# Row products by table, bias and batch in one matmul, token groups in serpentine order, and a new order of pieces behind the sort

## The chip, the cores and the metric

The kernel runs on one core of one Trainium2 chip. The metric is the device time of one execution in microseconds (us). Three runs of the kernel before took 981.32, 984.67 and 981.96 us; their median is 981.96. One further execution was recorded by the hardware profiler: it took 977.43 us, and its profile is what the prediction reads.

The engines are named as in the profile: PE (TensorE: matrix products), PEld (its weight loads), DVE (VectorE), ACT (ScalarE), POOL (GpSimd, which here also issues the indirect DMAs that gather rows), and SP (SyncE, which here only issues DMAs).

## The reference, cut to what matters

`x` is 16 batches of 512 tokens of 512 numbers, all float32. Each token has a pathway (of 500), a compartment c (of 5), and a mask value m (0 or 1, in a table of three scales).

```python
def _ln(x, g, b): return (x - mean(x)) * rsqrt(var(x) + 1e-5) * g + b
def _mlp_ln(s, W1, b1, W2, b2, g, b): return _ln(silu(s @ W1 + b1) @ W2 + b2, g, b)

h = _ln(x, pw_g[pathway], pw_b[pathway])
h = _ln(h, cp_g[c], cp_b[c])
t = _ln(x, tm_g[c], tm_b[c])
s = _ln(x, ms_g[m], ms_b[m])
mem, noi, res = (x + _mlp_ln(state, ...)[:, None, :] for each of three states of the batch)
w = softmax(aw)                                            # six weights
cat = concat([w[0]*h, w[1]*t, w[2]*mem, w[3]*noi, w[4]*res, w[5]*s])   # 3072 wide
out = x + _mlp_ln(cat, int_W1, int_b1, int_W2, int_b2, int_g, int_be)
```

## The kernel before, in words

The 8192 tokens are 64 tiles of 128; four tiles are a window, and there are 16 windows. `D` is 512, cut into `NC` = 4 blocks of 128.

**The first layer by groups.** The tables of `t` and `s` depend on (m, c) alone. There are `NR3` = 3 by `NR5` = 5, `NG` = 15 groups (the mask takes two of the three). The kernel sorts all tokens by group on the chip (a loop of one-hot products on PE, L710 to L733) and then gathers each tile of sorted tokens by an indirect DMA on POOL. The tokens of a tile then mostly share their group, so the weights of `t` and `s` with their gains can be one 512 by 512 block per tile, `vs`: ACT scales `ws` (`s_part`, `sp`, L213) and DVE adds the scaled `wt` (`build`, `bd`, L222). So `layer1` (L315) has three blocks of four matmuls for each tile: X (the tokens, against the summed weights of the three states, `wx_`), V (the normalized tokens against `vs`) and H (the twice normalized tokens against `wh_`). The pieces are `lX`, `lV`, `lH`.

**What is added to the rows.** What depends on the batch (16, through the three states) and on the group, and the bias `b1`, is one of 240 rows (`NB1` = 15 x 16). They are made in two halves of `HB` = 120 (`rows_product`, `rp`, L1071): one matmul of a one-hot `pick` against the summed tables `br2`, four matmuls against the identity that bring the bias (`b1r`), and one matmul of another one-hot against the batch rows `br`. `br2` is the copy (`br2`, L999) of what `table_products` (`tb`, L992) summed up; `br` is the copy (`cr`, L1042) of what `cond_product` (`cm`, L1035) summed up from the states; both copies are on ACT. The halves are copied (`rc`) and written by SP to two tables in memory, `rows_1` and `rows_2` (`ro`, L1082); the rows of a tile are gathered from `rows_2` (`ga`, L228) and added behind layer 1 (`ha`, L323).

**Extra tiles.** Where a group ends within a tile, the tile is built with the weights of one group, and the tokens of the other are corrected. The 15 groups have 14 boundaries. Half tiles of 64 tokens at the boundaries are put together in pairs, two to an extra tile, plus one (`ex.0`, against `ws`) for the two boundaries between mask values, where c changes too: `NX` = 7, and eight extra tiles, in two sets e0 and e1 of up to four. Each is gathered (`gx`), normalized, multiplied by the difference of the two groups' gains (`gr`, `mt`), turned (`tr`, `sE`), and multiplied by `wt` or `ws` (`extra`, `ex`, L1097: four matmuls). The product is added to the gathered rows (`ea`, `ee`) and written to `rows_1` or `rows_2` (`extra_out`, `eo`, L1110), from where the corrected tokens gather it by the indices that `kinds` (L891), `extra_adds` (L1057) and `add_rows` (`ar`, L1116) work out.

**Turning.** The products need the tokens' numbers on the partitions. DVE transposes 32 by 32 (`turn`, L182; pieces `tx`, `tv`, `th`, `tz`), and SP moves the 64 KB strips into place (`spread_row`, L187): one row group of a block is a piece `sX`, `sV`, `sH` or `sZ` with four DMAs. In window 0, X is turned by PE instead (`xt`, copies `xv`).

**The second layer** is seven products of quarters for each two tiles (`seventh`, `q7`, L397) with sums and differences of the turned rows on POOL (`zs`, L375), or plainly four matmuls a tile (`layer2`, `l2`, L336) in the first windows and the last.

**The order.** No scheduler decides it: each engine gets its instructions in the order of three written lists. `ORDER` holds the start, up to and into the first windows; `WINDOW` is run for w = 0 to 14 with the suffixes o, p, c, n and m for the windows w-2, w-1, w, w+1 and w+2 (a piece that ran already is left out); `LAST` is the last window and the end. In a piece, `lX.c.2` is block X of layer 1 for tile 2 of the current window. Pieces in `ORDER` that are not layer work: `lw` loads `w2` (L1140), `wm` sums its columns on ACT (`w2_means`, L1129: six ACT instructions), `wk` weighs `wx_` on DVE, `wh` weighs `wh_` on ACT (L979), `xs` are the row sums of a tile on ACT, `nv` and `xn` its two norms, `fn` and `fp` the second norm of H.

## Time and profile before

| | us |
|---|---|
| three runs | 981.32, 984.67, 981.96 |
| profiled execution | 977.43 |
| its span (first to last instruction) | 975.6 |
| PE busy | 951.4 |
| PE weight loads busy | 500.4 |
| DVE busy | 811.8 |
| POOL busy | 661.9 |
| ACT busy | 573.8 |

The granted clock of PE is 0.992 of full speed over the span. A busy PE need not be PE at its peak, since the ends of its pipelined matmuls are modelled. The profile counts a float32 matmul as two instructions. A row of the time line has start, duration, engine, line, operation, output and inputs by the program's names, sizes and the number of instructions taken together; a bracket at its end names the wait ahead of it. A row of the stretches has the stretch, its length, the busy time of PE, PEld, DVE, ACT and POOL with the number of instructions, PE's clock, the share of DMA time and GB/s. `SPq` is the queue in which SP issues DMAs. The 64 tiles need 504, 512 and 512 matmul instructions in blocks V, X and H of the first layer.

### The profile page before, as it was taken

The page shows a single profiled execution, that of the slowest core. Times are in us where ns is not written, and L with a number is a line of the kernel's source. Part 1 is how long each engine was busy: PE and PEld are TensorE (multiplying, and loading weights), DVE is VectorE, ACT ScalarE, POOL GpSimd, SP SyncE. Part 2 cuts the span into 40 slices and gives each one's busy share as a digit, 9 for nine tenths or more (in the row PEclk, how much of TensorE's full clock was granted, in tenths as well). Part 3 has the DMA queues.
Part 4 walks back from the last instruction along what each step waited for, and adds up shares of the span by engine and source line. Part 5 has one row for each costly group of instructions (what it writes and reads, how often), then busy time and mean ns, then how long its engine had stood idle before and what let it go on. Part 6 is the DMA issues. An engine that isn't in the chain of part 4 may idle for free. (4 is left out here: it accounts for less than half of the span.)

```text
span 975.6 us, 11492 instructions
## 1 busy us (share of the span) xinstructions
PE 951.4 (98%) x2921; PEld 500.4 (51%) x2921; DVE 811.8 (83%) x1402; ACT 573.8 (59%) x1190; POOL 661.9 (68%) x683
## 2 busy tenths in 40 slices
...
GB/s 277 211 259 236 270 262 217 147 228 192 206 189 184 190 196 168 213 202 193 227 189 203 176 197 174 198 183 195 215 195 219 186 185 188 198 180 190 131 84 97
DMA packets 92044, 191.47 MB, mean 196 GB/s; under 512 B 25332, under 2 KB 25332, under 8 KB 91980
## 3 DMA queue, kind: packets, MB, share of 16 engines
...
## 5 line engine op out<-in xcount | busy, mean ns | idle before, releaser
L320 PE MATMUL p<-vs,cV 128*128 128x512 f32 x504 | 225.7, 592 | 0.0
L320 PE MATMUL p<-wx__82,cX 128*128 128x512 f32 x512 | 224.9, 592 | 0.0
L320 PE MATMUL p<-wh__83,cH 128*128 128x512 f32 x512 | 223.3, 592 | 0.8 <-DMA cH<-rH 0.7
L226 DVE SCALAR_TENSOR_TENSOR vs<-wt,sct,vs 128x512 f32<-128x512 f32 x252 | 186.8, 805 | 1.6 <-ACT vs L220 1.6
L220 ACT ACTIVATE vs<-ws,scs 128x512 f32<-128x512 f32 x252 | 164.0, 711 | 7.6 <-PE p L320 3.6
L320 PEld LDWEIGHTS p<-wh__83,cH 128*128 128x128 f32 x512 | 97.1, 190 | 123.9 <-issue 118.0
L320 PEld LDWEIGHTS p<-wx__82,cX 128*128 128x128 f32 x512 | 97.2, 190 | 122.8 <-issue 116.4
L320 PEld LDWEIGHTS p<-vs,cV 128*128 128x128 f32 x504 | 95.8, 190 | 109.5 <-issue 93.0
L497 POOL DMA_INDIRECT out<-yb,tok x64 | 80.1, 1251 | 71.5 <-DVE yb L462 21.9
L471 ACT ACTIVATE junk<-yb 128x512 f32<-128x512 f32 x64 | 40.4, 631 | 116.0 <-DVE yb L435 92.4
L327 ACT ACTIVATE add<-add 128x512 f32<-128x512 f32 x64 | 39.4, 626 | 93.9 <-DVE add L324 93.9
L158 POOL DMA_INDIRECT add<-rows,i_add x64 | 73.6, 1149 | 19.4 <-issue 10.4
L158 POOL DMA_INDIRECT pw<-in_pw,i_pw x64 | 71.8, 1122 | 19.6 <-issue 16.9
L309 POOL TENSOR_TENSOR xbs<-xbs,rows 128x512 f32<-128x512 f32 x64 | 84.0, 1313 | 1.0
L158 POOL DMA_INDIRECT xbs<-in_x,tok x64 | 67.1, 1049 | 25.7 <-issue 12.3
L158 POOL DMA_INDIRECT cp<-cp_rows,i_cp x64 | 63.0, 984 | 20.5 <-issue 18.6
L260 ACT ACTIVATE xm<-xbs,nmx,rsx 128x512 f32<-128x512 f32 x64 | 51.7, 810 | 38.1 <-DVE rV L184 38.1
L484 POOL TENSOR_TENSOR rsy<-vey,mhalf 128x4 f32<-128x4 f32 (+1 forms) x15 | 21.3, 1423 | 77.4 <-DVE vey L479 77.3
L283 DVE TENSOR_TENSOR pw<-xn,pw 128x512 f32<-128x512 f32 x64 | 45.5, 710 | 26.5 <-DMA pw<-in_pw,i_pw 26.2
L238 ACT ACTIVATE junk<-xbs 128x512 f32<-128x512 f32 x72 | 44.9, 623 | 33.2 <-DMA xbs<-in_x,tok 30.9
L292 POOL TENSOR_TENSOR rsh<-veh,mhalf 128x1 f32<-128x1 f32 x64 | 43.3, 681 | 25.9 <-DVE vea L244 16.4
L296 ACT ACTIVATE pw<-pw,rsh 128x512 f32<-128x512 f32 x64 | 44.1, 711 | 27.5 <-POOL rsh L292 27.3
...
## 6 DMA issues: line engine op xcount, KB each, us to landing
cV<-rV SPq DMA_DIRECT2D x256, 64.0 KB
cH<-rH SPq DMA_DIRECT2D x256, 64.0 KB
cZ<-rZ SPq DMA_DIRECT2D x256, 64.0 KB
cX<-rX SPq DMA_DIRECT2D x240, 64.0 KB
...
```

The lines of the kernel that those rows point to most:

```text
L158: nc.gpsimd.indirect_dma_start(dst, None, table, bass.IndirectOffsetOnAxis(ap=idx, axis=0), **kw)
L220: nc.scalar.activation(v[:, c], ws[:, c], AF.Identity, scale=scs[:, c, g, w : w + 1])
L226: nc.vector.scalar_tensor_tensor(v[:, c], wt[:, c], sct[:, c, g, w : w + 1], v[:, c], ALU.mult, ALU.add)
L238: nc.scalar.activation(junk, x, AF.Identity, accum_out=sums[:, 0, j : j + 1])
L260: nc.scalar.activation(t, st["xb"][:, j, :], AF.Identity, bias=st["nm"][:, j : j + 1], scale=st["rs"][:, j : j + 1])
L283: nc.vector.tensor_mul(pw[:, :D], st.pop(("xn", j)), pw[:, :D])
L292: nc.gpsimd.tensor_tensor(rs, st.pop(("ve", j)), mhalf[:, :1], ALU.pow)
L296: nc.scalar.mul(pw[:, :D], pw[:, :D], st.pop(("rs", j)))
L309: nc.gpsimd.tensor_add(st["xb"][:, j, :], st["xb"][:, j, :], rows[:, 2, :])
L320: nc.tensor.matmul(st["p1", g], st["c" + blk][:, g, c, :], m[:, c, :], start=(blk == "X" and c == 0), stop=(blk == "H" and c == NC - 1))
L471: nc.scalar.activation(junk, yb[:, j, :], AF.Square, accum_out=st["ssy"][:, j : j + 1])
L497: nc.gpsimd.indirect_dma_start(out_rows, bass.IndirectOffsetOnAxis(ap=tok[:, j, w : w + 1], axis=0), yb[:, j, :], None)
```

## The change

It has three parts.

1. The tables, the bias and the batch rows are summed in one PSUM tile, `pb`. The columns of the tables are moved behind the 16 of the batches, a fourth plane of `tabs` holds the bias in column L - 1 = 31, and four matmuls of 32 by 128 against the identity add it. The copy `br2` is gone, `cr` copies all; `pick` is a single one-hot sum with up to four ones in a column, and `rows_product` is one matmul for each half. `cond_affine` now works on 16 of the 32 columns.

2. The groups are ordered as a serpentine: where m is odd, c runs backwards. At the boundary between two mask values c is then the same on both sides. `NX` becomes 6, there are seven extra tiles (`ex.0` to `ex.6`), and `rows_2` holds 14 half tiles behind the 240 rows. `extra_out` writes two halves for each extra tile to `rows_2`, the first one to `rows_1` as well. The index patterns `i_grp` and `of_*` are made in more pieces, and `kinds` and `add_rows` have more small steps.

3. `ORDER` behind the one-hot loop and `WINDOW` are new; `LAST` is the same. In the new `ORDER` the pieces `lw`, `wm`, the early `xt` and the gathers of the extra tokens stand earlier; `cr` now has `wm` ahead of it. In the new `WINDOW`, `tz.p.3` stands behind `bd.c.1`, and `sZ.p.3` ahead of `sZ.p.2` and `sZ.p.1`.

```diff
 ORDER = """
-    sz scl bx lt ax wk.1.3 h2.1 ac sp.0.0 h2.2 lh he.2 cv h2.0 he.0 wk.1.1 pk se eh.2 eh.0 lw by pwi kd px dk he.1
-    eh.1 wk.1.0 gh.0.2 xs.0.1 xs.0.0 dp wk.1.2 tk xt.0.2 xt.0.3 cg gh.0.0 gh.0.1 xs.0.3 xt.0.1 cs wk.2.2 xv.0.2
-    xt.0.0 cp gx.e1.3 gx.e0.1 tt wk.2.0 cn xs.0.2 xv.0.3 xe.0 xv.0.1 dc wh gx.e1.2 xp.0 xv.0.0 ct xm.0 xn.0.2
-    gx.e0.0 ca f1.0.2 nv.0.1 xn.0.1 wk.2.1 tb br2 fp.0.2 cm do xn.0.0 wk.2.3 lX.0.1 gx.e0.2 f2.0.2 f1.0.0 fp.0.0
-    nv.0.2 fn.0.2 xs.e0.1 xn.0.3 lo lX.0.3 tv.0.2 nv.0.0 nv.0.3 th.0.2 gh.0.3 lX.0.0 tv.0.1 cr rp.1 f2.0.0 fn.0.0
-    f1.0.1 tv.0.0 tv.0.3 xs.e0.0 fp.0.1 f2.0.1 th.0.0 xs.e0.2 sp.0.1 gx.e0.3 xs.e0.3 gr.e0.2 sV.0.2 f1.0.3 gx.e1.0
...
+    sz scl bx lt ax wk.1.3 h2.1 wk.1.0 ac lw wk.1.1 se xt.0.0 by h2.2 pwi dk lh sp.0.0 gh.0.1 gh.0.0 xt.0.1 kd
+    bd.0.0 cv he.1 xv.0.1 xv.0.0 dp px tt gh.0.2 xs.0.0 wk.1.2 wk.2.3 tk xs.0.1 h2.0 gx.e0.0 wk.2.1 eh.1 pk he.2
+    xs.0.3 xs.0.2 xe.0 wk.2.2 xt.0.2 wk.2.0 xp.0 xt.0.3 he.0 dc wh xm.0 gx.e0.2 xv.0.2 nv.0.1 xv.0.3 nv.0.2 eh.0
+    xn.0.2 eh.2 tb cs xn.0.1 xs.e0.0 nv.0.0 tv.0.1 lX.0.3 lX.0.0 gx.e0.3 gx.e0.1 f1.0.2 do gx.e1.1 tv.0.2 cp xn.0.0
+    f1.0.0 gx.e1.0 cn fp.0.2 f2.0.2 ct xs.e0.3 xs.e0.1 f2.0.0 cg gx.e1.3 gr.e0.3 fp.0.0 f1.0.1 xs.e0.2 gr.e0.1 lo
+    xe.e0 ca xp.e0 tv.0.0 nv.0.3 wm gx.e1.2 gr.e0.0 xm.e0 nv.e0.3 xn.0.3 nv.e0.0 lX.0.2 tv.0.3 cm gr.e0.2 nv.e0.1
+    gh.0.3 f2.0.1 gx.1.0 fn.0.0 mt.e0.3 gr.e1.2 fp.0.1 tr.e0.3 lX.0.1 mt.e0.1 sV.0.0 th.0.0 sV.0.1 cr rp.0 nv.e0.2
+    tr.e0.1 mt.e0.0 tr.e0.0 wl.3 sp.0.1 mt.e0.2 rc.0 xs.e1.3 xs.e1.1 tr.e0.2 fn.0.1 fn.0.2 xs.e1.2 gx.1.3 rp.1
+    bd.0.1 f1.0.3 gr.e1.1 xs.e1.0 lV.0.0 f2.0.3 fp.0.3 sV.0.3 gr.e1.3 xa lV.0.1 sE.e0.3 xe.e1 th.0.2 xp.e1 rc.1
+    fn.0.3 xm.e1 sp.0.3 nv.e1.2 nv.e1.3 gx.1.2 xs.1.0 th.0.3 sh.0.2 sE.e0.1 ex.3 gx.1.1 ex.1 sE.e0.0 sE.e0.2 ex.0
+    ro.1 nv.e1.1 th.0.1 tx.1.3 ex.2 ro.0 xs.1.2 sV.0.2 mt.e1.3 sH.0.3 sH.0.0 xs.1.3 gx.2.2 tr.e1.3 bd.0.3 wl.2 wl.1
+    gx.2.1 ea.0 tx.1.2 gr.e1.0 mt.e1.2 xs.1.1 gh.1.0 nv.e1.0 tx.1.1 xe.1 tr.e1.2 sH.0.2 xp.1 sH.0.1 mt.e1.0 mt.e1.1
...
 WINDOW = """
-    xn.c.3 ha.p.3 hs.p.3 tz.p.3 xs.n.0 lX.c.0 lV.c.0 lb.o.3 lX.c.2 tz.p.2 xn.c.2 sZ.p.0 sZ.p.2 gx.n.2 gx.n.3 xs.n.1
-    xs.n.2 sp.c.2 po.o.2 xs.n.3 gh.n.1 lX.c.3 lX.c.1 f1.c.3 f2.c.3 fp.c.3 bd.c.1 lV.c.1 ga.c.0 po.o.3 bd.c.2 sp.c.3
-    sZ.p.1 f1.c.2 fp.c.2 xe.n q7.p.1.1 lV.c.2 tx.n.3 xp.n sZ.p.3 fn.c.3 zs.p.0 zs.p.4 zs.p.1 f2.c.2 zs.p.2 tx.n.2
-    kf.p.2 xm.n xn.n.0 q7.p.0.1 nv.n.3 q7.p.0.2 tx.n.1 tx.n.0 zs.p.5 zs.p.6 zs.p.7 th.c.3 fn.c.2 tv.n.3 kf.p.0
-    xn.n.1 th.c.2 q7.p.0.5 sh.c.0 q7.p.0.6 sf.p.0 gh.n.0 kf.p.1 q7.p.1.6 q7.p.1.5 sX.n.2 ku.p.1 bd.c.3 q7.p.1.2
-    sX.n.1 sH.c.0 nv.n.0 zs.p.3 q7.p.0.7 ga.c.1 kf.p.3 sf.p.1 q7.p.1.7 tv.n.0 q7.p.1.3 sf.p.3 nv.n.2 sH.c.1 q7.p.0.4
-    f1.n.0 f1.n.1 sH.c.2 nv.n.1 sh.c.3 tv.n.2 ga.c.2 q7.p.1.4 ku.p.0 q7.p.0.3 sf.p.2 sl.p.0 sp.n.0 lV.c.3 sX.n.3
-    lH.c.1 ga.c.3 sl.p.2 lH.c.0 gh.n.3 sh.c.1 sl.p.3 sl.p.1 tv.n.1 bd.n.0 lq.p.3 lq.p.2 lq.p.0 lq.p.1 lv.p lp.p
-    f2.n.0 f2.n.1 sp.n.1 sH.c.3 fp.n.1 sX.n.0 fp.n.0 lb.p.1 ha.c.0 po.p.1 lb.p.0 fn.n.0 th.n.0 ha.c.1 sV.n.0 gx.m.1
-    fn.n.1 hs.c.0 lH.c.2 ha.c.2 th.n.1 sV.n.2 lH.c.3 gx.m.0 tz.c.0 sV.n.1 po.p.0 sV.n.3 gh.n.2 lb.p.2 sh.c.2 hs.c.1
-    hs.c.2 tz.c.1
+    lX.c.3 lX.c.0 ha.p.3 hs.p.3 ga.c.2 lV.c.0 tz.p.2 xn.c.3 lb.o.3 gx.n.3 bd.c.1 xs.n.0 xn.c.2 po.o.2 sh.c.3 tz.p.3
+    xs.n.1 lX.c.1 lV.c.1 gx.n.2 gh.n.1 lX.c.2 f1.c.2 sp.c.2 sp.c.3 xs.n.3 f2.c.2 sZ.p.0 f1.c.3 f2.c.3 sZ.p.3 bd.c.2
+    lV.c.2 fp.c.3 fn.c.3 th.c.3 fp.c.2 po.o.3 ga.c.1 sZ.p.2 bd.c.3 xs.n.2 sZ.p.1 xe.n xp.n q7.p.1.1 zs.p.4 fn.c.2
+    th.c.2 sH.c.1 zs.p.0 zs.p.1 sp.n.0 sH.c.0 xm.n nv.n.1 tv.n.1 tx.n.2 q7.p.0.1 tx.n.1 zs.p.5 xn.n.1 q7.p.0.2
+    lV.c.3 kf.p.0 nv.n.3 kf.p.2 q7.p.0.5 tx.n.0 tx.n.3 kf.p.1 q7.p.1.5 zs.p.6 sH.c.3 sh.c.0 zs.p.7 f1.n.1 q7.p.1.6
+    nv.n.0 tv.n.3 sX.n.3 q7.p.0.7 ku.p.1 zs.p.2 q7.p.1.2 sf.p.2 kf.p.3 bd.n.0 q7.p.1.7 nv.n.2 tv.n.2 sH.c.2 f2.n.1
+    q7.p.0.6 q7.p.1.3 sX.n.1 sf.p.3 lH.c.1 ga.c.0 sh.c.1 tv.n.0 ha.c.1 lH.c.0 sl.p.2 ku.p.0 sf.p.1 sl.p.0 ha.c.0
+    zs.p.3 gh.n.0 q7.p.1.4 q7.p.0.4 gh.n.2 hs.c.1 xn.n.0 sl.p.3 lq.p.2 sf.p.0 lq.p.3 q7.p.0.3 sl.p.1 hs.c.0 sX.n.0
+    fp.n.1 lq.p.0 sh.c.2 fn.n.1 f1.n.0 lq.p.1 ga.c.3 lv.p tz.c.1 fp.n.0 lH.c.2 sp.n.1 th.n.1 ha.c.2 f2.n.0 lp.p
+    lb.p.1 sV.n.3 gh.n.3 hs.c.2 sV.n.1 po.p.1 lb.p.0 gx.m.0 sV.n.2 gx.m.1 sV.n.0 fn.n.0 lH.c.3 tz.c.0 lb.p.2 sX.n.2
+    po.p.0 th.n.0
...
-    NX = NG // 2
+    NX = (NG - NR3) // 2
...
-    rows_2 = dram.tile([NB1 + NX * P, D], F32, name="rows_2")
+    rows_2 = dram.tile([NB1 + (NG - 1) * (P // 2), D], F32, name="rows_2")
...
-    i_grp = iota(prep.tile([P, NG], F32, name="i_grp"), [[1, NG]])
+    i_grp = prep.tile([P, NG], F32, name="i_grp")
+    for m in range(NR3):
+        back = m % 2
+        iota(i_grp[:, m * NR5 : (m + 1) * NR5], [[1 - 2 * back, NR5]], base=m * NR5 + back * (NR5 - 1))
...
-    nc.gpsimd.tensor_scalar(w_c, w_m, -float(NR5), 1.0, ALU.mult, ALU.add)
-    n_x = prep.tile([P, 3, 2 * Q], F32, name="n_x")
+    turns, past_half, step_back = [prep.tile([P, 1], F32, name=n) for n in ("turns", "past_half", "step_back")]
+    nc.gpsimd.tensor_scalar(w_c, w_m, -1.0, 1.0, ALU.mult, ALU.add)
+    for k in range(1, NR3):
+        nc.gpsimd.tensor_scalar(turns, i_row, float(k * NR5 - 1 + k % 2), 2.0 - 4.0 * (k % 2), ALU.is_ge, ALU.mult)
+        nc.gpsimd.tensor_add(w_c, w_c, turns)
+    nc.gpsimd.tensor_scalar(past_half, i_row, float(P // 2), None, ALU.is_ge)
+    nc.gpsimd.tensor_scalar(step_back, past_half, -float(P), float(P // 2), ALU.mult, ALU.add)
+    n_x = prep.tile([P, 3, NX + 1], F32, name="n_x")
     d_x = prep.tile([P, 2, 2 * Q], F32, name="d_x")
+    nc.gpsimd.memset(d_x, 0.0)
...
-    tabs = scratch(0, 3, NC, L)
+    tabs = scratch(0, 4, NC, L)
...
-    def pairs(pattern, base):
-        t = scratch(1, NB1)
-        iota(t.rearrange("p (m c b) -> p m c b", m=NR3, c=NR5), pattern, base=base)
-        return t
-
-    of_batch = pairs([[0, NR3], [0, NR5], [1, B]], 0)
-    of_c = pairs([[0, NR3], [1, NR5], [0, B]], 0)
-    of_m = pairs([[1, NR3], [0, NR5], [0, B]], NR5)
+    of_batch, of_c, of_m = [scratch(1, NB1) for _ in range(3)]
+    for t, v in ((of_batch, 0), (of_c, 1), (of_m, 2)):
+        for m in range(NR3):
+            back = m % 2
+            pattern, base = (([[0, NR5], [1, B]], 0), ([[1 - 2 * back, NR5], [0, B]], B + back * (NR5 - 1)),
+                             ([[0, NR5], [0, B]], B + NR5 + m))[v]
+            iota(t[:, m * NR5 * B : (m + 1) * NR5 * B].rearrange("p (c b) -> p c b", c=NR5), pattern, base=base)
...
-            nc.sync.dma_start(tabs[:, k, :, lo:hi], a[nm].rearrange("(c p) r -> p c r", p=P))
+            nc.sync.dma_start(tabs[:, k, :, B + lo : B + hi], a[nm].rearrange("(c p) r -> p c r", p=P))
...
+        cc, cb = [prep.tile([P, 2, NX + 1], F32, name=n) for n in ("cc", "cb")]
+        for k in range(1, NR3, 2):
+            nc.vector.tensor_scalar(cb, cc, -2.0, float(NR5 - 1), ALU.mult, ALU.add)
+            nc.vector.scalar_tensor_tensor(cb, mm, float(k), cb, ALU.is_equal, ALU.mult)
+            nc.vector.tensor_add(cc, cc, cb)
...
+        nc.vector.tensor_copy(tabs[:, 3, :, L - 1 :], b1c[:, 3, :].unsqueeze(2))
...
     def table_products():
-        at_["pbt"] = pbt = psum(1, "pbt")
+        at_["pb"] = pb = psum(1, "pb")
         for k, m in enumerate((wt, ws, wh_)):
             for c in range(NC):
-                nc.tensor.matmul(pbt[c * L : (c + 1) * L], tabs[:, k, c, :], m[:, c, :],
-                                 start=(k == 0), stop=(k == 2))
-
-    def table_rows():
-        at_["br2"] = gp.tile([P, D], F32, tag="add", name="br2", bufs=4)
-        nc.scalar.copy(at_["br2"], at_["pbt"])
+                nc.tensor.matmul(pb[c * L : (c + 1) * L], tabs[:, k, c, :], m[:, c, :], start=(k == 0), stop=False)
+        for c in range(NC):
+            nc.tensor.matmul(pb[c * L : (c + 1) * L, c * P : (c + 1) * P], tabs[:, 3, c, :], ident,
+                             start=False, stop=False)
...
     def cond_affine():
-        nc.vector.tensor_mul(hTc, at_["pt"], gb[:, :, :, 1:2].to_broadcast([P, NC, 3, L]))
-        nc.vector.tensor_add(hTc, hTc, gb[:, :, :, 2:3].to_broadcast([P, NC, 3, L]))
+        h = hTc[:, :, :, :B]
+        nc.vector.tensor_mul(h, at_["pt"][:, :, :, :B], gb[:, :, :, 1:2].to_broadcast([P, NC, 3, B]))
+        nc.vector.tensor_add(h, h, gb[:, :, :, 2:3].to_broadcast([P, NC, 3, B]))
 
     def cond_product():
-        at_["pb"] = pb = psum(1, "pb")
+        pb = at_["pb"]
         for s in range(3):
             for c in range(NC):
                 nc.tensor.matmul(pb[c * L : (c + 1) * L], hTc[:, c, s, :], w1x[s][:, c, :],
-                                 start=(s == 0), stop=(s == 2))
+                                 start=False, stop=(s == 2))
...
-        at_["pick"] = pick = gp.tile([P, D], F32, tag="add", name="pick", bufs=4)[:, : 2 * NB1].rearrange(
-            "p (v n) -> p v n", v=2)
-        nc.vector.tensor_scalar(pick[:, 0], of_batch, inq, None, ALU.is_equal)
-        nc.vector.tensor_scalar(pick[:, 1], of_c, inq, None, ALU.is_equal)
-        nc.vector.scalar_tensor_tensor(pick[:, 1], of_m, inq, pick[:, 1], ALU.is_equal, ALU.add)
-        at_["b1r"] = b1r = gp.tile([P, D], F32, tag="add", name="b1r", bufs=4)[:, : NC * HB].rearrange(
-            "p (c n) -> p c n", c=NC)
-        nc.vector.tensor_copy(b1r, b1c[:, 3, :].unsqueeze(2).to_broadcast([P, NC, HB]))
+        at_["pick"] = pick = gp.tile([P, D], F32, tag="add", name="pick", bufs=4)[:, :NB1]
+        last = small.tile([P, 1], F32, tag="last", name="last", bufs=1)
+        nc.vector.tensor_scalar(last, inq, float(L - 1), None, ALU.is_equal)
+        nc.vector.tensor_scalar(pick, of_batch, inq, last, ALU.is_equal, ALU.add)
+        nc.vector.scalar_tensor_tensor(pick, of_c, inq, pick, ALU.is_equal, ALU.add)
+        nc.vector.scalar_tensor_tensor(pick, of_m, inq, pick, ALU.is_equal, ALU.add)
...
     def rows_product(h):
         at_["pr", h] = pr = psum(1, f"pr{h}")[:HB]
-        nc.tensor.matmul(pr, at_["pick"][:, 1, h * HB : (h + 1) * HB], at_["br2"], start=True, stop=False)
-        for c in range(NC):
-            nc.tensor.matmul(pr[:, c * P : (c + 1) * P], at_["b1r"][:, c, :], ident, start=False, stop=False)
-        nc.tensor.matmul(pr, at_["pick"][:, 0, h * HB : (h + 1) * HB], at_["br"], start=False, stop=True)
+        nc.tensor.matmul(pr, at_["pick"][:, h * HB : (h + 1) * HB], at_["br"], start=True, stop=True)
...
     def extra_out(k):
         if k == 0:
             nc.sync.dma_start(rows_1[NB1:, :], at_["adde", k])
-        else:
-            nc.sync.dma_start(rows_2[NB1 + (k - 1) * P : NB1 + k * P, :], at_["adde", k])
+        H = P // 2
+        at = [b for b in range(NB) if (b % NR5 == NR5 - 1) == (k == 0)][2 * max(k - 1, 0) :]
+        for v in range(2):
+            nc.sync.dma_start(rows_2[NB1 + at[v] * H : NB1 + (at[v] + 1) * H, :], at_["adde", k][v * H : (v + 1) * H])
...
+        g1 = g0.rearrange("p g w -> p (g w)")
+        com, turn_ = [prep.tile([P, Q * NW], F32, name=n) for n in ("com", "turn_")]
+        off = com
+        nc.vector.tensor_scalar(off, g_n, past_half, None, ALU.subtract)
+        nc.vector.tensor_scalar(turn_, off, float(NR5 - 1), None, ALU.is_equal)
+        for k in range(2, NR3):
+            nc.vector.scalar_tensor_tensor(turn_, off, float(k * NR5 - 1), turn_, ALU.is_equal, ALU.add)
+        nc.vector.tensor_sub(off, g_n, g1)
+        nc.vector.tensor_mul(off, off, off)
+        nc.vector.scalar_tensor_tensor(turn_, off, 1.0, turn_, ALU.not_equal, ALU.mult)
+        nc.vector.scalar_tensor_tensor(own, turn_, step_back, own, ALU.mult, ALU.add)
```

65 lines of the change are left out of this document (29 added, 36 removed).

## The prediction, made before the run

> **What bounds the kernel now.** I read the page's head first, then the waits of PE, then the time line of PE through the start, then one steady window.
>
> ```profile
> span 975.6 us, 11492 instructions
> PE 951.4 (98%) x2921; PEld 500.4 (51%) x2921; DVE 811.8 (83%) x1402; ACT 573.8 (59%) x1190; POOL 661.9 (68%) x683
> PE pc L651 <- DVE sm L657: 6.7, 1, 6.7
> PE p L320 <- DMA cH<-rH: 0.7, 1, 0.7
> PE p L339 <- DMA cZ<-rZ: 0.6, 1, 0.6
> 945.45 20.61 PE p L339 x48
> ```
>
> The first row is the span. The profiled execution took 977.43 us, so 1.83 us lie around it. PE is busy for 951.4 of 975.6 us. In the rows of the waits (engine, line, what ended the wait, total, number, longest) nothing exceeds 6.7 us, and that one lies ahead of the sort, where nothing is changed. The last row, from the chain that ended last, puts PE's end at 945.45 + 20.61 = 966.06; the 9.5 us behind it are the last output, in a list that is not edited. So the end is set by PE, if it is fed.
>
> ```profile
> 480.00:540.00 60.00, 60.00 (x174) 31.80 (x173) 52.34 (x92) 38.14 (x78) 42.51 (x42) 1.00 0.72 204
> 518.41 3.60 PE L320 MATMUL p<-wx__82,cX 128*128 128x512 f32 x8
> 539.01 0.27 PE L404 MATMUL pq_1a<-b2r,share 96*128 96x256 bf16 x1
> ```
>
> The first row is a stretch of steady windows (length, then busy time of PE, PEld, DVE, ACT and POOL, the granted clock, DMA share, GB/s): PE 60.00 of 60.00, clock 1.00, DVE 52.34. There an order of pieces cannot gain, only lose. The other two rows (start, duration) are the first block of the second window's end and the first product behind it. Six layer blocks (each one tile by one 512-wide part of the first layer, four matmuls recorded as eight instructions) lie between 518.41 and 539.01: 20.60 / 6 = 3.43 us each. That is PE's price of one unit of dense work, and the unit in which I count everything that PE is spared.
>
> ```profile
> 36.00:42.00 6.00, 6.00 (x83) 4.69 (x85) 3.77 (x18) 2.91 (x10) 4.81 (x4) 0.64 0.41 115
> 48.00:54.00 6.00, 3.82 (x21) 1.93 (x20) 5.72 (x16) 5.71 (x17) 4.35 (x5) 1.00 1.01 365
> 54.00:60.00 6.00, 5.73 (x40) 1.69 (x44) 4.72 (x10) 5.54 (x9) 3.13 (x4) 0.72 1.00 328
> 61.69 10.57 PE L320 MATMUL p<-wx__82,cX 128*128 128x512 f32 x24
> 80.71 7.03 PE L320 MATMUL p<-vs,cV 128*128 128x512 f32 x16
> ```
>
> The first three rows have the same columns as the stretch above. Behind the sort PE's work is small products, at a clock of 0.64 in the first stretch and 1.00 and 0.72 in the others, where ACT is busy for 5.71 and 5.54 of 6.00 us. From 61.69 on PE runs dense layer blocks. I take 80.71 as the mark: both row products are done, and the blocks on V and H follow.
>
> **The change part by part.**
>
> *Row products.* `rows_product` loses its table matmul and four bias matmuls; one matmul is left.
>
> ```profile
> 72.10 1.02 PE L1073 MATMUL pr<-br,pick 128*120 128x512 f32 x2
> 73.83 1.02 PE L1076 MATMUL pr<-br,pick 128*120 128x512 f32 x2
> 74.69 3.60 PE L320 MATMUL p<-wx__82,cX 128*128 128x512 f32 x8
> ```
>
> A half takes 72.10 to 74.69, 2.59 us: the table group and the bias group (four matmuls of 128 columns, in the trace between the two rows shown) 72.10 to 73.83, 0.865 each, and the batch group 0.86. One group stays: 2 x (2.59 - 0.86) = 3.46 us less. `table_products` gains four matmuls of 32 by 128 against the identity. No row shows them; the nearest is the bias group (0.87), bounds 0.2 (a quarter, if the four strips ran side by side) and 0.87. I take 0.87. Net 2.59 on PE; by PE's queue alone the mark comes at 80.71 - 2.59 = 78.1.
>
> *Extra tiles.* NX falls from 7 to 6, and the program's order has seven products `ex` instead of eight.
>
> ```profile
> 112.49 20.83 PE L1100 MATMUL pe<-wt,cEe 128*128 128x512 f32 x48
> 133.16 3.60 PE L320 MATMUL p<-wh__83,cH 128*128 128x512 f32 x8
> ```
>
> Six take 112.49 to 133.16, 3.45 us each. One fewer: 3.45 us off a stretch where PE is dense. DVE, POOL and the gathers lose a piece each, which nobody waits for.
>
> *The head's new order.* Here PE is not alone. The copy of the summed table, `cr`, stands on ACT, and both row products wait for it. I sum ACT's queue up to it in the new order.
>
> ```profile
> 40.51:68.72 28.21, 25.76 (x153) 9.71 (x146) 22.30 (x56) 22.37 (x45) 17.80 (x18) 0.87 0.81 265
> 40.51 2.56 ACT L220 ACTIVATE vs<-ws,scs 128x512 f32<-128x512 f32 x4
> 43.84 0.58 ACT L956 COPY ev<-po 128x512 f32<-128x512 f32 x1 [0.78 <-PE po L952]
> 46.79 0.63 ACT L238 ACTIVATE junk<-xbs 128x512 f32<-128x512 f32 x1
> 48.62 0.63 ACT L238 ACTIVATE junk<-xbs 128x512 f32<-128x512 f32 x1
> 54.01 0.67 ACT L927 ACTIVATE dr<-pdr,w_d 34x512 f32<-34x512 f32 x1
> 54.58 1.99 ACT L980 ACTIVATE wh__83<-wh__83,wx 128x2048 f32<-128x2048 f32 x1
> 57.39 0.80 ACT L260 ACTIVATE xm<-xbs,nmx,rsx 128x512 f32<-128x512 f32 x1
> 58.10 0.80 ACT L260 ACTIVATE xn<-xbs,nmx,rsx 128x512 f32<-128x512 f32 x1
> 64.89 0.63 ACT L238 ACTIVATE junk<-xbs 128x512 f32<-128x512 f32 x1 [1.94 <-DMA xbs<-in_x,tok_x]
> 68.72 0.56 ACT L1044 COPY br<-pb 128x512 f32<-128x512 f32 x1
> 109.51 0.64 ACT L1133 ACTIVATE junk<-w 128x512 f32<-128x512 f32 x1
> 113.50 0.81 ACT L260 ACTIVATE xn<-xbs,nmx,rsx 128x512 f32<-128x512 f32 x1
> ```
>
> The first row is the stretch between the first V weights and `cr` in the run before; the others are start, duration and, in brackets, what ended the wait ahead. From 40.51: four activations for the first V weights 2.56; three copies `ev` at 0.58, 1.74; eight tiles of row sums at 1.83 (46.79 to 48.62), 14.64; `dr` 0.67; the weighing of `wh_` 1.99; eleven norms at 0.71 (57.39 to 58.10), 7.81; one `fn`, bounded by the same 0.71; and `wm`, 3.99 (109.51 to 113.50). That one used to run at 109 and now stands ahead of `cr`: it is the price of this order. Sum 34.1, so 74.6 without waits. Before, ACT was idle for 28.21 - 22.37 = 5.84 us of that stretch; the largest single wait is 1.94 (in the row of 64.89, for the gather of the extra tokens). Bounds 0 and 5.84; I take 1.94, since that gather stays on the path while the load `lw` moves ahead of it. `cr` begins at 76.55, ends at 77.1, and the two products (0.86 each) put the mark at 78.8: later than PE's own 78.1, so ACT decides, 1.9 us earlier than 80.71. Bounds: 76.9 (no waits, and PE early enough) and 82.7 (all of them). Behind `cr` on ACT stand the scales of the second V weights, and PE's second V block waits for them; it comes one block after the mark.
>
> *Added DMAs and small work.* `extra_out` writes each tile in halves: 15 issues on SP instead of 8. The queue is nearly full there.
>
> ```profile
> 92.79 13.19 SPq L192 DMA_DIRECT2D cEe<-rEe  x16
> 122.08 1.70 SPq L1114 DMA_DIRECT2D rows<-adde  x3
> ```
>
> Seven more at 1.70 / 3 = 0.57 are +4.0; the fourth row group of the second extra set falls away, four issues at 13.19 / 16 = 0.82, -3.3. Net +0.7 on SP, whose lateness PE showed as 0.72 and 0.60 (the two DMA waits above). For later stalls of PE I take +0.2, bounds -1.3 (both waits vanish) and +3 (another row group, 4 x 0.82, late). The new small instructions ahead of the sort go to POOL:
>
> ```profile
> 35.60 2.37 POOL L158 DMA_INDIRECT xbs<-in_x,tok  x1 [7.72 <-DVE room L780]
> ```
>
> The bracket says that it idles 7.72 us there, until DVE has sorted, so the new index patterns and turns, on one column or 240, are covered as long as they stay under that sum; beyond it the gather of the first tokens at 35.60 would start late. DVE gets three small steps in `kinds` and seven in `add_rows`, and loses a copy in `pick_rows`; they are one column or 128 short rows wide, far narrower than the 512 of the transposition shown below at 0.70, and DVE has a rest of 60.00 - 52.34 = 7.66 us per 60 even in the steady part, so I cost them at nothing; without that rest they would be ten at 0.2 to 0.70, 2 to 7 us of DVE, and the V weights behind them on DVE would be late.
>
> *The window's new order.* WINDOW is reordered too, and runs 13 times with full layer blocks. The tightest step is PE's first product of the second layer. It needs the third group of `cZ` instead of the second, and `tz.p.3`, which completes the source, now stands behind `bd.c.1`.
>
> ```profile
> 526.90 0.70 DVE L184 STREAM_TRANSPOSE rZ<-add 128x512 f32<-128x512 f32 x1
> 530.62 5.38 DVE L226 SCALAR_TENSOR_TENSOR vs<-wt,sct,vs 128x512 f32<-128x512 f32 x8
> 473.81 10.82 SPq L192 DMA_DIRECT2D cZ<-rZ  x16
> 527.67 11.94 SPq L192 DMA_DIRECT2D cZ<-rZ  x16
> 488.01 1.42 POOL L383 TENSOR_TENSOR zs<-cZ 128x256 f32<-128x256 f32 x2 [1.69 <-DMA cZ<-rZ]
> ```
>
> Before, the last such transposition ends at 527.60, 9.2 after the window's first block. Four builds are 5.38 / 2 = 2.7: now 11.9. Twelve issues at 0.68 to 0.75 (the two rows of `cZ`, by 16) are 8.1 to 9.0, and the landing adds 488.01 - 484.63 = 3.4: 23.4 to 24.3. PE is there after seven blocks, 24.0. So the slack is from +0.6 to -0.3. DVE started the chain earlier in its own queue, so I take no stall, bounds 0 and 0.3 x 13 = 3.9.
>
> Sum: -1.9 - 3.45 + 0.2 + 0 = -5.15. Profiled 977.43 becomes 972.3. The runs shown have a median 4.53 above it, 981.96; I carry the difference over: 976.8.
>
> The Trainium skill, "TensorE: Matmul & The Clock Gate", section "Part 4: PE-mode transpose", says that PE transposes do not count as activity for the clock. This order brings two tiles' transposes forward among the cold products, so by that rule the dense part begins cold. The stretch at 48.00, in which PE turned tiles among its products too, had a clock of 1.00 and does not bear it out. By the rule the start would cost what the fourth rival costs.
>
> **The rivals.**
> 1. The head gains all: no wait on ACT (mark 76.9, -3.8) and no later DMA wait (-1.3): 981.96 - 3.8 - 3.45 - 1.3 = 973.4. For it: `lw` moves to a time when DMA is 0.41 busy. Against: ACT is full already.
> 2. The row products were hidden: `cr` late by the full 5.84, mark 82.7 (+2.0): 981.96 + 2.0 - 3.45 + 0.2 = 980.7, and with 3 of later stalls 983.5. For it: `wm` now stands ahead of it. Against: before, the same gathers cost ACT at most 1.94 in one place.
> 3. Slower: `cZ` lands late in every window. At 1 us each, 13 windows: 976.8 + 13 = 989.8. It makes the kernel measurably slower from (5.15 + 2.95) / 13 = 0.62 us per window, and eats the gain from 0.40. For it: a slack of half a microsecond. Against: a stall would move PE's later blocks and with them DVE's start, and 0.62 is beyond my bound of 0.3.
> 4. The clock stays low at the dense start: a stretch of 6 us at 0.72 (as at 54.00) instead of 1.00 costs 1.7, if ACT is not later anyhow: 978.5.
>
> **How the numbers follow.** My forecast (976.8, itself 975 to 980) gets 0.54, the rivals 0.14, 0.14, 0.13 and 0.05. A measurement of this kernel tells 0.3%, 2.95 us, from no change: faster is below 979.0, slower above 984.9. Faster: 0.46 of the forecast's 0.54, all of the first rival, 0.03 of the fourth: 0.63. Slower: 0.11 of the third and 0.01 of the second: 0.12. The rest, 0.25, is the same. The range: 973.4 less the scatter of the three runs at the low end, 972; at the high end the second rival's 983.5, rounded up to 984.
>
> **What would show it.** Right: seven `ex` products; two row products of 0.9 us that begin at the end of `cr`; the mark (both row products done) at 77 to 81; steady stretches like that at 480.00, with PE busy throughout and the first `b2r` products of successive windows as far apart as now. The step on ACT is wrong if PE waits before the row products for something else, the step on SP if waits on `cH`, `cV` or `cEe` exceed 3 us. The window step is wrong if PE shows a wait on `cZ` at the first product of layer 2 in each window, and the forecast is wrong altogether if the period grows by more than 0.40.

## The result, and the profile after

Eighteen runs of the kernel after have a median of 974.01 us (970.42 to 981.2), eighteen runs of the kernel before 980.78 (974.49 to 988.13): ratio 0.9947, 95% interval 0.9926 to 0.9967. The forecast was 976.8 against 981.96, also 0.9947. That ratio stands for 5.2 us; the two medians are 6.8 us apart. The profiled execution took 971.0 us (before 977.43). The sum came out right, but several of its terms did not, as the parts below show. The profiled execution of the kernel after is the third shortest of its eighteen runs and the one of its repetition on a second chip the second shortest of twelve, while those of the kernel after with the old ORDER list are near its medians, so that a span of one profile must not be set against a median.

First the head of the page after, the waits of PE (engine, line, what ended the wait, total, number, longest), and a row of the chain that ended last:

```profile
span 969.1 us, 11569 instructions
PE 942.4 (97%) x2901; PEld 497.7 (51%) x2901; DVE 820.2 (85%) x1412; ACT 571.5 (59%) x1190; POOL 653.1 (67%) x697
...
PE p L320 <- DVE adde L1118: 2.9, 1, 2.9
PE pdr L938 <- DVE cX L960: 2.3, 1, 2.3
PE p L320 <- DMA cH<-rH: 1.7, 3, 0.8
PE pe L1110 <- DMA cEe<-rEe: 1.2, 1, 1.2
...
938.98 20.61 PE p L339 x48
```

PE ends at 938.98 + 20.61 = 959.59, before at 966.06: 6.47 us earlier, and the 9.5 us behind it are unchanged. The waits have moved: none is left in the windows, but three groups of them (2.9, 1.7 and 1.2 us) lie behind the row products, where before had 0.7, 0.6 and 0.6.

The time line of PE through the start of the kernel after:

```profile
59.02 7.13 PE L320 MATMUL p<-wx__82,cX 128*128 128x512 f32 x16
...
66.33 3.62 PE L320 MATMUL p<-wx__82,cX 128*128 128x512 f32 x8
...
72.59 3.70 PE L320 MATMUL p<-wx__82,cX 128*128 128x512 f32 x8
76.41 1.98 PE L1086 MATMUL pr<-br,pick 128*120 128x512 f32 x4
78.22 7.03 PE L320 MATMUL p<-vs,cV 128*128 128x512 f32 x16
86.45 7.10 PE L1110 MATMUL pe<-wt,cEe 128*128 128x512 f32 x16 [1.20 <-DMA cEe<-rEe]
...
142.91 3.70 PE L320 MATMUL p<-wx__82,cX 128*128 128x512 f32 x8 [2.93 <-DVE adde L1118]
```

The two row products are done at 78.22 (before 80.71; forecast 78.8): 2.49 us. They are 1.81 us from start to start of the next, where before they were 2 x 2.59. The first extra product now comes behind two V blocks, where before it came behind six blocks, and waits 1.20 for its strips; the X block at 142.91 waits 2.93 until DVE has freed an accumulator (a PSUM tile that collects a product).

The copy `cr` in ACT's time line, then PE's stretches (length, busy time of PE, PEld, DVE, ACT, POOL, granted clock, DMA share, GB/s):

```profile
75.79 0.56 ACT L1059 COPY br<-pb 128x512 f32<-128x512 f32 x1
```

```profile
36.00:42.00 6.00, 6.00 (x85) 4.15 (x83) 3.46 (x14) 3.12 (x11) 4.86 (x4) 0.76 0.77 251
42.00:48.00 6.00, 3.70 (x25) 1.61 (x22) 5.76 (x20) 5.84 (x15) 4.68 (x5) 0.96 0.81 240
48.00:54.00 6.00, 5.32 (x50) 2.65 (x50) 5.19 (x13) 4.60 (x13) 5.17 (x4) 0.61 1.01 334
480.00:540.00 60.00, 60.00 (x176) 32.15 (x175) 52.47 (x88) 38.09 (x79) 41.05 (x42) 1.00 0.71 202
```

PE's fourth X block (72.59 + 3.70 = 76.29) and the copy (75.79 + 0.56 = 76.35) end together. The clock at 48 to 54 us is 0.61, where before it was 1.00. And the steady stretch is as full as before. In the kernel before, other stretches were not as full as this one. Two rows of PE's waits in the kernel before, at products of the second layer in the windows, for POOL's sums and for the strips of Z:

```profile
PE pq_1a L406 <- POOL zs L387: 0.9, 4, 0.3
PE pq_1a L406 <- DMA cZ<-rZ: 0.6, 2, 0.3
```

The distance between windows shows the whole delay. The group of the first `b2r` products, one for each of 13 windows, in the kernel before (durations in ns, then first and last start in us):

```profile
L404 PE MATMUL pq_1a<-b2r,share x13: 274/274/274, 214.0 to 863.3; 96*128 96x256 bf16 x13
```

and in the kernel after:

```profile
L404 PE MATMUL pq_1a<-b2r,share x13: 275/275/276, 216.1 to 861.0; 96*128 96x256 bf16 x13
```

Twelve distances took 863.3 - 214.0 = 649.3 us before, 54.11 each; after, 644.9, or 53.74 each. So 4.4 us of the gain lie in the windows.

The accounts, by the profiled executions. Up to the first `b2r` product both kernels have 38 layer-sized products on PE behind the mark (before 10 V, 8 H, 8 X, 4 of layer 2 and 8 extra; after 11 V, 8 H, 8 X, 4 and 7). At 3.433 us each these are 130.5 us. Before they take 213.96 - 80.71 = 133.3, a loss of 2.8; after, 216.11 - 78.22 = 137.9, a loss of 7.4. Of the 7.4, 5.8 are the waits above (2.9 for DVE's addition, 1.7 for strips of H, 1.2 for strips of the extra tokens).

| part | forecast | by the profile |
|---|---|---|
| both row products done | -1.9 | -2.49 |
| one extra product less | -3.45 | -3.43 |
| stalls of PE from there to the first `b2r` product | +0.2 | 7.4 - 2.8 = +4.6 |
| the twelve windows | 0 | -4.4 |
| the last windows (what is left of the difference at PE's end) | 0 | -0.8 |
| sum | -5.15 | -6.5 |

Two terms that are off by 4 to 5 us in opposite directions cancel: that the forecast was met is luck in these two terms. Which part of the change each belongs to, the profile can't say, since three edits meet in it.

### The profile page after: what moved, and what is told of

Read it like the earlier page. It is cut to its first block, busy times and chain, and to the rows that moved or that the text cites. A ratio compares the mean times of both kernels' runs of the same rounds, so it can differ in the third digit from the quotient of the medians.

```text
span 969.1 us, 11569 instructions
## 1 busy us (share of the span) xinstructions
PE 942.4 (97%) x2901; PEld 497.7 (51%) x2901; DVE 820.2 (85%) x1412; ACT 571.5 (59%) x1190; POOL 653.1 (67%) x697
## 4 chain that ended last, share of the span: by engine, by line
PE 84%; DVE 6%; DMA 5%; issue 2%; POOL 1%; SPq 1%; ACT 0%; POOLq 0%; ACTq 0%; DVEq 0%
PE p L320 62%; PE pq_0b L406 5%; PE pq_1b L406 5%; PE p L339 4%; PE pq_1a L406 3%; PE pq_0a L406 3%; DMA cH<-rH 2%; SPq L192 1%; DMA pw<-in_pw,i_pw 1%; DMA cX<-rX 1%; DVE vs L724 1%; POOL xbs L158 1%; DVE pw L283 0%; DMA pre<-diff_rows,tok_x 0%; DVE vs L226 0%
## 5 line engine op out<-in xcount | busy, mean ns | idle before, releaser
L320 PE MATMUL p<-wx__82,cX 128*128 128x512 f32 x512 | 227.9, 593 | 2.9 <-DVE adde L1118 2.9
L320 PE MATMUL p<-wh__83,cH 128*128 128x512 f32 x512 | 225.8, 593 | 1.8 <-DMA cH<-rH 1.7
L226 DVE SCALAR_TENSOR_TENSOR vs<-wt,sct,vs 128x512 f32<-128x512 f32 x252 | 175.8, 758 | 0.4 <-ACT vs L220 0.4
L497 POOL DMA_INDIRECT out<-yb,tok x64 | 71.5, 1116 | 76.4 <-DMA out<-yb,tok 27.9
L309 POOL TENSOR_TENSOR xbs<-xbs,rows 128x512 f32<-128x512 f32 x64 | 81.7, 1279 | 0.8
L158 POOL DMA_INDIRECT add<-rows,i_add x64 | 69.0, 1078 | 16.6 <-issue 14.8
L324 DVE TENSOR_TENSOR add<-p,add 128x512 f32<-128x512 f32 x64 | 43.0, 673 | 24.7 <-PE p L320 24.6
L301 DVE SCALAR_TENSOR_TENSOR pw<-pw,mvh,cp 128x512 f32<-128x512 f32 x64 | 60.4, 944 | 0.0
```

What stands on the lines that cost most here:

```text
L158: nc.gpsimd.indirect_dma_start(dst, None, table, bass.IndirectOffsetOnAxis(ap=idx, axis=0), **kw)
L226: nc.vector.scalar_tensor_tensor(v[:, c], wt[:, c], sct[:, c, g, w : w + 1], v[:, c], ALU.mult, ALU.add)
L301: nc.vector.scalar_tensor_tensor(pw[:, :D], pw[:, :D], mv[:, 0, 0:1], cp, ALU.subtract, ALU.mult)
L309: nc.gpsimd.tensor_add(st["xb"][:, j, :], st["xb"][:, j, :], rows[:, 2, :])
L320: nc.tensor.matmul(st["p1", g], st["c" + blk][:, g, c, :], m[:, c, :], start=(blk == "X" and c == 0), stop=(blk == "H" and c == NC - 1))
L324: nc.vector.tensor_add(st["add", g], st["p1", g], st["add", g])
```

## The experiments

Each exchanges a list or a part between the two kernels. The ratio is of run times to the kernel before on the same chip, with its 95% interval. "V" is the start of the first V block (the mark, where nothing waits), "loss" is the time from there to the first `b2r` product less the products' 3.433 us each (37 to 39, by the lists), "windows" is the excess of the twelve distances over 12 x 53.74, all in us and from one profiled execution each. V depends on PE's clock in the start as well, which differs between executions, so that V alone tells little of a kernel.

| kernel | ratio | V | loss | windows |
|---|---|---|---|---|
| before | 1 | 80.7 | 2.8 | 4.4 |
| after | 0.9947 (0.9926 to 0.9967) | 78.2 | 7.4 | 0.0 |
| after, second chip | 0.9962 (0.9938 to 0.9985) | 80.7 | 7.8 | 0.4 |
| before, new WINDOW | 0.9915 (0.9888 to 0.9942) | 83.3 | 1.3 | 0.1 |
| after, old WINDOW | 1.0040 (1.0006 to 1.0075) | 81.4 | 12.9 | 0.0 |
| after, old ORDER | 0.9895 (0.9869 to 0.9920) | 82.3 | 4.7 | 1.6 |
| the same, second chip | 0.9898 (0.9880 to 0.9917) | 81.6 | 4.1 | 2.5 |
| after, both old lists | 0.9910 (0.9879 to 0.9940) | 82.0 | 6.7 | 1.5 |
| before, row products in one | 0.9993 (0.9967 to 1.0018) | 81.8 | 3.5 | 10.7 |
| before, serpentine | 0.9934 (0.9907 to 0.9960) | 82.8 | 3.4 | 2.2 |
| after, `ee.5` earlier | 0.9944 (0.9928 to 0.9960) | 82.4 | 10.0 | 0.0 |
| after, `wm` later | 0.9980 (0.9955 to 1.0006) | 82.3 | 11.6 | 0.2 |
| after, `bd.0.0` later | 0.9947 (0.9914 to 0.9980) | 82.0 | 13.7 | 0.0 |
| after, both moved | 0.9968 (0.9944 to 0.9991) | 81.5 | 13.8 | 0.0 |

**The two lists.** The old WINDOW list in the kernel after:

```diff
 WINDOW = """
-    lX.c.3 lX.c.0 ha.p.3 hs.p.3 ga.c.2 lV.c.0 tz.p.2 xn.c.3 lb.o.3 gx.n.3 bd.c.1 xs.n.0 xn.c.2 po.o.2 sh.c.3 tz.p.3
...
+    xn.c.3 ha.p.3 hs.p.3 tz.p.3 xs.n.0 lX.c.0 lV.c.0 lb.o.3 lX.c.2 tz.p.2 xn.c.2 sZ.p.0 sZ.p.2 gx.n.2 gx.n.3 xs.n.1
```

> The kernel after with the WINDOW list of before; all else as after. Theory A (the new window list itself took time out of the 13 steady windows): the mean distance of successive first b2r products goes back from 53.74 to about 54.1 us, the end comes 4.5 to 5.2 us later, profiled span about 974; both row products still done at 78.2. Rival B (the windows of before were longer because the old head handed its delays on, the list is neutral): distance 53.74, span 969 to 970.

The median is 983.25 (before 983.25), and five of its twelve runs took 990 to 994 us. The profiled execution is the shortest of the twelve, 980.99, with a span of 979.2, well above the 974 of theory A. Its group of first `b2r` products:

```profile
L404 PE MATMUL pq_1a<-b2r,share x13: 275/275/276, 221.3 to 866.2; 96*128 96x256 bf16 x13
```

Twelve distances of 53.74 again, as rival B has it. Yet the kernel is slower, as theory A has it, by another way: in this execution the loss sits ahead of the first `b2r` product, 12.9 us. What the runs of 990 to 994 us add, no profile shows. A wait in its time line of PE, at the end of that part:

```profile
205.78 12.23 PE L320 MATMUL p<-wx__82,cX 128*128 128x512 f32 x24 [3.00 <-DMA cX<-rX]
```

The new list in the kernel before is the same diff turned round.

> The kernel before with the WINDOW list of after; all else as before. Theory A: distance of the first b2r products 53.74 in every window, span 975.6 - 5 = about 970.5; both row products done at 80.7 as before. Rival B: distance still up to 55 in the first windows, span 975 to 976.

```profile
L404 PE MATMUL pq_1a<-b2r,share x13: 274/274/274, 218.5 to 863.5; 96*128 96x256 bf16 x13
```

The median falls from 983.25 to 975.11, by 8.1 us (5.7 to 11.0 by the interval): more than the 4.4 that the profile before showed in the windows. The whole change has 0.9947 on other chips, and the intervals overlap, so the list alone is worth about as much as the whole change. Theory A's outcome holds: the list gains behind the old head too, and the distances are even. Rival B falls here.

The old ORDER in the kernel after, without the pieces that no longer exist:

```diff
 ORDER = """
-    sz scl bx lt ax wk.1.3 h2.1 wk.1.0 ac lw wk.1.1 se xt.0.0 by h2.2 pwi dk lh sp.0.0 gh.0.1 gh.0.0 xt.0.1 kd
...
+    sz scl bx lt ax wk.1.3 h2.1 ac sp.0.0 h2.2 lh he.2 cv h2.0 he.0 wk.1.1 pk se eh.2 eh.0 lw by pwi kd px dk he.1
```

> The kernel after with the ORDER list of before, without the copy of the table sums, the eighth extra tile's pieces and the fourth row group of the second extra set, which the program no longer has; window list, row products and serpentine as after. Theory C (the new head order costs: behind the mark PE loses 7.4 us against 2.8 before): PE loses about 2.8 between the mark and the first b2r product, both row products are done at about 78.1, span 969.1 - 4.6 = about 964.5. Rival D (the serpentine's seven extra tiles and their half writes bring the stalls, whatever the order): loss 6 to 7.5 again, span about 969. Rival E (the old order cannot feed PE that early, the 2.59 us saved on PE turn into waits ahead of the mark): mark 80 to 81, span 967.

Measured 0.9895, 974.08 us: faster than the kernel after. PE's time line:

```profile
78.79 1.02 PE L1086 MATMUL pr<-br,pick 128*120 128x512 f32 x2
82.27 8.80 PE L320 MATMUL p<-vs,cV 128*128 128x512 f32 x16 [2.46 <-DMA cV<-rV]
```

The row products are done at about 79.7, and the first V block waits 2.46 us for its strips: the wait that rival E named. The two V blocks then take 8.80 us, where the kernel after has 7.03. The loss behind V is 4.7 (theory C had 2.8, rival D 6 to 7.5). The profiled span is 972.2, far from theory C's 964.5 and longer than the 969.1 of the profile of the kernel after: the gain shows in the run times, and not between these two profiles. A second chip was to settle whether the two ratios may be compared, since they came from different chips:

> The kernel after, unedited, on the same chip as the kernel after with the ORDER list of before, since their ratios to before came from different chips. Theory C (the new head order costs): ratio to before about 0.995, 4 to 5 us above the next kernel. Rival F (the two chips differ in what they grant PE at the start, and the head order is worth nothing): both ratios the same, about 0.99 or 0.995.

> The kernel after with the ORDER list of before, without the pieces that are gone; the same kernel as in the first group. Theory C: ratio to before about 0.9895 again, below the kernel after by 4 to 5 us. Rival F: the same as the kernel after.

979.74 against 973.04 us on one chip, intervals apart. Theory C's outcome holds: the new head order costs 6.7 us at the median (0.9962 - 0.9898 = 0.0064 by the ratios, 6.3 us). One run of the kernel after in this group took 2306.84 us at a mean clock of 0.41; the ratio does not rest on it. Where the 6.7 us lie, the two profiles don't show: their spans are 972.3 and 971.7. The mean clocks of the runs differ: the other eleven of the kernel after have 0.983 to 0.990, median 0.986, the five with the old ORDER 0.989 to 0.992, median 0.990. By the 0.87 us for each 0.001 of clock that the last section works out, this difference is 3.5 us, an estimate; the rest stays open.

With both old lists:

> The kernel after with both lists of before (ORDER without the pieces that are gone): the row products in one matmul and the serpentine alone. Theories A and C: 964.5 + 5 = about 969.5 span, that is 3.4 (one extra product) and 2.6 (row products) below the 975.6 of before. Rival D: about 974. If both merely shift waits: 975.

0.9910, 974.95 us. The row products and the serpentine by themselves bring 8.3 us at the median; the 6.0 expected lies at the lower end of the interval, 5.9 to 11.9.

**The two parts alone.** The row products in one matmul, in the kernel before:

```diff
-        nc.tensor.matmul(pr, at_["pick"][:, 1, h * HB : (h + 1) * HB], at_["br2"], start=True, stop=False)
-        for c in range(NC):
-            nc.tensor.matmul(pr[:, c * P : (c + 1) * P], at_["b1r"][:, c, :], ident, start=False, stop=False)
-        nc.tensor.matmul(pr, at_["pick"][:, 0, h * HB : (h + 1) * HB], at_["br"], start=False, stop=True)
+        nc.tensor.matmul(pr, at_["pick"][:, h * HB : (h + 1) * HB], at_["br"], start=True, stop=True)
```

> The kernel before with the row products by table, bias and batch in one matmul alone (the copy of the table sums falls away); eight extra tiles, both lists as before. Theory G (what is taken off PE's queue ahead of 80 us shortens the run): by PE's queue 2.59 us, so 0.997 of before, with both row products done at 78.1. Rival E (the time saved turns into a wait for the V strips that SP moves): both done at 78 to 79.5, but the first V block starts at 80 to 82 as before, ratio 1.000. Rival H (not additive: with a head that is less late the old windows run at 53.74 at once): ratio 0.992, as much as the window list alone.

```profile
64.15 10.57 PE L320 MATMUL p<-wx__82,cX 128*128 128x512 f32 x24
78.84 1.02 PE L1071 MATMUL pr<-br,pick 128*120 128x512 f32 x2
81.81 7.11 PE L320 MATMUL p<-vs,cV 128*128 128x512 f32 x16 [1.95 <-DMA cV<-rV]
L404 PE MATMUL pq_1a<-b2r,share x13: 274/275/276, 215.7 to 871.3; 96*128 96x256 bf16 x13
```

No gain is seen: 0.9993. Its interval, 0.9967 to 1.0018, shuts out rival H, but it reaches down to theory G's 0.997, so that the time alone does not decide between G and E. Rival E's mechanism is in the rows. PE is through with the row products before 79.9, and then waits 1.95 us for the V strips, where the kernel before did not wait. The start at 81.81 can't be set against 80.71 by itself, since the X blocks of this execution began 2.5 us later (64.15 against 61.69). From the first X block to the first V block it is 17.66 us against 19.02, so 1.36 us earlier, and not the 3.46 by which PE's products in between are shorter. Its windows are 10.7 us too long, in the kernel before 4.4 under the same list: the delays under the old list differ much between profiles.

The serpentine alone, in the kernel before (the row products as before):

```diff
-    NX = NG // 2
+    NX = (NG - NR3) // 2
...
-    i_grp = iota(prep.tile([P, NG], F32, name="i_grp"), [[1, NG]])
+        iota(i_grp[:, m * NR5 : (m + 1) * NR5], [[1 - 2 * back, NR5]], base=m * NR5 + back * (NR5 - 1))
```

> The kernel before with the serpentine order alone: seven extra tiles, half writes, the longer index work; row products in six matmuls each and both lists as before, without the eighth extra tile's pieces. Theory K (the serpentine brings nearly all that it and the row products bring together, which was 0.991): ratio 0.990 to 0.993, that is more than the one product of 3.45 us (0.9965), because PE and SP are both one tile ahead when the windows begin and their distances fall to 53.74. Rival L (one product and no more): 0.9965. Rival M (neither gains alone, since the row products alone gave 0.999): 0.998 to 1.000.

```profile
L404 PE MATMUL pq_1a<-b2r,share x13: 274/274/275, 213.2 to 860.3; 96*128 96x256 bf16 x13
```

0.9934 is 6.5 us. That lies just above theory K's range; the interval, 0.9907 to 0.9960, covers most of that range, and rival L's 0.9965 lies just above the interval: the product of 3.43 us, and some of the old list's excess (2.2 in place of 4.4, by one profile of each). As theory K has it, the distances are 53.74, all but the first, which is 55.90. The half writes, seven more issues on SP against four fewer strips, are not seen to cost anything.

**Within the new head.** Three pieces in the start could be the price; each was moved. First the addition that frees the accumulator for the X block at 142.91:

```diff
-    xs.2.0 ea.4 sh.0.0 tv.1.0 fp.1.2 sh.1.2 xs.2.3 eo.6 eo.3 f1.1.1 sp.1.0 f2.1.2 ee.5 xe.2 lX.1.1 fp.1.1 sX.1.2
+    xs.2.0 ea.4 sh.0.0 tv.1.0 ee.5 fp.1.2 sh.1.2 xs.2.3 eo.6 eo.3 f1.1.1 sp.1.0 f2.1.2 xe.2 lX.1.1 fp.1.1 sX.1.2
```

> The kernel after with one piece moved: the addition that frees the fifth extra product's accumulator (ee.5) stands behind tv.1.0 and so ahead of f1.1.1, sp.1.0 and f2.1.2 of window 1; all else as after. Theory I (the new list has put this addition too late on DVE, and a layer block waits for its accumulator): PE's wait of 2.9 us for it at 142.9 goes, no other wait replaces it, the end comes 2.9 us earlier, 0.997 of the kernel after. Rival J (the next wait, for an H strip at 160 to 164, takes it over): the wait goes and the end stays, 0 to 1 us.

```profile
150.91 1.98 PE L320 MATMUL p<-vs,cV 128*128 128x512 f32 x4 [2.99 <-DVE vs L226]
```

The X block no longer waits, and the V block behind it waits 2.99 us for its weights from DVE. Neither theory I nor J named that heir; theory I falls with it, since it had no other wait in its place. The time does not decide: 977.74 us against 979.74 for the kernel after on that chip, 2.0 us between the 2.9 of theory I and the 0 to 1 of rival J, with intervals that overlap (0.9944 and 0.9962). In this execution the lateness passes to DVE's next piece for PE. It isn't there every time: in the profile of the kernel after on the second chip, PE waits 0.4 us for that addition in place of 2.9.

Then the step on which the prediction put the row products, ACT's sums of `w2`:

```diff
-    xe.e0 ca xp.e0 tv.0.0 nv.0.3 wm gx.e1.2 gr.e0.0 xm.e0 nv.e0.3 xn.0.3 nv.e0.0 lX.0.2 tv.0.3 cm gr.e0.2 nv.e0.1
+    xe.e0 ca xp.e0 tv.0.0 nv.0.3 gx.e1.2 gr.e0.0 xm.e0 nv.e0.3 xn.0.3 nv.e0.0 lX.0.2 tv.0.3 cm gr.e0.2 nv.e0.1
...
-    tr.e0.1 mt.e0.0 tr.e0.0 wl.3 sp.0.1 mt.e0.2 rc.0 xs.e1.3 xs.e1.1 tr.e0.2 fn.0.1 fn.0.2 xs.e1.2 gx.1.3 rp.1
+    tr.e0.1 mt.e0.0 tr.e0.0 sp.0.1 mt.e0.2 rc.0 xs.e1.3 xs.e1.1 tr.e0.2 fn.0.1 fn.0.2 xs.e1.2 gx.1.3 rp.1
+    wm wl.3 bd.0.1 f1.0.3 gr.e1.1 xs.e1.0 lV.0.0 f2.0.3 fp.0.3 sV.0.3 gr.e1.3 xa lV.0.1 sE.e0.3 xe.e1 th.0.2 xp.e1 rc.1
```

> The kernel after with the column sums of w2 (wm, 3.9 us of ACT, and wl.3 that needs them) behind the second row product instead of ahead of cr; all else as after. Theory N, the prediction's (ACT's queue up to cr decides when both row products are done): they are done 2 to 3.5 us earlier, at 75 to 77 where the clock at 36 to 48 us is 0.76 and 0.96, and 77.5 to 78.5 where it is 0.5 and 0.7. Rival O (PE comes there no earlier itself: in the profiles of after its fourth X block ends within 0.2 us of the copy): 0 to 0.3 us, ratio to the kernel after 1.000.

PE's row products, and the copy in ACT's time line:

```profile
80.58 1.88 PE L1086 MATMUL pr<-br,pick 128*120 128x512 f32 x4
```

```profile
78.45 0.56 ACT L1059 COPY br<-pb 128x512 f32<-128x512 f32 x1
```

The copy now ends at 79.01, and the products still begin at 80.58: PE itself is late. Rival O's mechanism holds, and the prediction's step on ACT falls: in the first profile of the kernel after, too, PE's X block ended with the copy, so ACT held PE by 0.1 us at most. The ratio, 0.9980, shows no gain; the kernel after was not run on this chip. What holds PE earlier, by its waits, are the copies `cX` on DVE, with a weight build ahead of them. That build was moved:

```diff
-    bd.0.0 cv he.1 xv.0.1 xv.0.0 dp px tt gh.0.2 xs.0.0 wk.1.2 wk.2.3 tk xs.0.1 h2.0 gx.e0.0 wk.2.1 eh.1 pk he.2
+    cv he.1 xv.0.1 xv.0.0 bd.0.0 dp px tt gh.0.2 xs.0.0 wk.1.2 wk.2.3 tk xs.0.1 h2.0 gx.e0.0 wk.2.1 eh.1 pk he.2
```

> The kernel after with the first weight build (bd.0.0, 2.74 us of DVE) behind the two copies xv.0.1 and xv.0.0 instead of ahead of them; all else as after. Theory O (PE decides, and it is held by its wait of 2.3 to 2.7 us for those copies at 44.9 to 50.6): the wait goes, PE's first X blocks start up to 2.3 us earlier; both row products then are done at most 0.3 us earlier as long as wm stands ahead of cr, 78 at a warm and 80.5 at a cold start. Rival: PE waits as long for the next thing (the copies ev on ACT), X blocks not earlier.

The waits of PE, the first X blocks, and a stretch ahead of them:

```profile
PE pdr L938 <- DVE cX L960: 0.5, 1, 0.5
PE hs L981 <- DVE tok_x L925: 1.1, 1, 1.1
PE po L967 <- ACT ev L971: 1.1, 1, 1.1
```

```profile
63.18 7.13 PE L320 MATMUL p<-wx__82,cX 128*128 128x512 f32 x16
```

```profile
54.00:60.00 6.00, 5.16 (x16) 2.32 (x20) 5.10 (x14) 5.31 (x10) 3.85 (x4) 0.50 0.87 260
```

The wait for `cX` is 0.5 in place of 2.3 to 2.8, and two waits of 1.1 stand in its place; the X blocks start at 63.18, where the kernel with `wm` later had them at 63.10. That is the rival's outcome. But the clock of 0.50 at 54 to 60 us takes up to 2.6 us by itself (half of the 5.16 us that PE is busy there, an estimate), so this profile can't show what the move is worth at a clock of 1. Both moves at once:

> Both moves at once: wm and wl.3 behind the second row product, bd.0.0 behind xv.0.0. If PE and ACT each held the row products alone (theories N and O together), they are done 2 to 2.5 us earlier than in the kernel after and its ratio falls by 0.002; if the stalls behind them (the first extra product waits for its strips, H strips late) take it all back, the row products are earlier and the time is that of the kernel after, about 0.995.

0.9968, the time of the kernel after within the intervals, and the row products are done at 81.5, not earlier (80.7 in the second execution of the kernel after). None of the three pieces that were moved carries the price of the new order by itself; the others were not tried.

One thing runs through the kernels of both heads: a long wait of PE is sometimes followed by a slow block. Time line of PE with both moves, and the stretch behind its longest wait there:

```profile
90.87 8.64 PE L1110 MATMUL pe<-wt,cEe 128*128 128x512 f32 x16 [2.35 <-DMA cEe<-rEe]
...
147.92 5.40 PE L320 MATMUL p<-wx__82,cX 128*128 128x512 f32 x8 [3.77 <-DVE adde L1118]
...
183.56 13.97 PE L339 MATMUL p<-w,cZ 128*128 128x512 f32 x32 [2.78 <-DMA cZ<-rZ]
```

```profile
147.90:151.50 3.60, 3.58 (x5) 1.49 (x6) 3.60 (x6) 1.61 (x3) 3.48 (x3) 0.60 0.64 143
```

After 3.77 us of waiting the clock is 0.60, and a block of 3.60 us takes 5.40. Two extra products after 2.35 us take 8.64, where the kernel after has 7.10 for two; the four blocks after 2.78 us are not slowed (13.97, 3.49 each). In the kernel after, the X block after 2.93 us took 3.70. The fourteen profiles have 24 waits of PE of 1.4 us or more behind the row products: none of the eight under 2.3 us is followed by such a slow block, six of the thirteen between 2.3 and 3.0 us are, and all three above 3.2 us. The Trainium skill, "TensorE: Matmul & The Clock Gate", section "Part 1: The HAM clock gate (the "warmup" mystery)", says that an idle array drops to half rate, and that it takes about 3.4 us of work, in windows that run freely, to come back; at half rate that costs about 1.7 us, an estimate from that page. The trace agrees on the price, 5.40 - 3.60 = 1.80, and on its chance, since waits of like length were punished in one place and not in another. It differs in one point: the same section puts the drop behind an idle window of about 3.4 us, and here waits of 2.35 to 3.00 us were enough in six cases.

## Why the prediction was right, and where it was not

*What bounds the kernel.* PE, and its last product sets the end: right, both kernels end 9.5 us behind it. "There an order of pieces cannot gain, only lose" is the step that failed, and with it the 0 for the windows in the sum. It was read from one stretch, 480 to 540 us, in which PE happened not to wait. The prediction asked whether the new list would bring a wait on `cZ`; it was the old list that had such waits. The distances of the same product over all windows, 54.11 on average against 53.74 there, stood in the same trace. In run times the list is worth 8.1 us behind the old head, and it makes the difference between 1.004 and 0.995 (on different chips) behind the new one.

*Row products.* The instructions went as counted. The four matmuls against the identity, priced at 0.87 us from the nearest row, take less. They stand here in the kernel after and in the one with `wm` later, where the next product starts 0.72 and 0.33 us behind them:

```profile
58.30 0.79 PE L1014 MATMUL pb<-ident,room 128*32 128x128 f32 x8
```

```profile
62.77 0.40 PE L1014 MATMUL pb<-ident,room 128*32 128x128 f32 x8
```

That the row products are worth 2.59 us "by PE's queue alone" did not reach the end of the run, as far as the runs tell: alone they give 0.9993, and in the profile the V blocks wait 1.95 us for strips that SP moves. The second rival had said that they were hidden; it named ACT's copy, and in that profile it was the strips.

*Extra tiles.* One product of 3.43 us, as forecast. Alone, the serpentine brings 6.5 (3.9 to 9.1 by its interval), and part of the rest is excess of the old windows.

*The new head, ACT.* 78.8 forecast, 78.22 measured, but not for the reason given: with `wm` out of the way PE begins no earlier. In the second execution of the same kernel, on another chip, the figure is 80.70, and the clock is the difference that shows:

```profile
36.00:42.00 6.00, 6.00 (x72) 5.51 (x72) 1.59 (x7) 1.41 (x7) 4.83 (x4) 0.50 0.84 267
42.00:48.00 6.00, 5.85 (x30) 1.90 (x26) 3.16 (x18) 3.78 (x9) 2.82 (x3) 0.71 0.66 198
78.98 1.88 PE L1086 MATMUL pr<-br,pick 128*120 128x512 f32 x4
80.70 7.34 PE L320 MATMUL p<-vs,cV 128*128 128x512 f32 x16
```

0.50 and 0.71 there, 0.76 and 0.96 in the execution above. That the number was met so closely is luck as well.

*Later stalls.* +0.2 with bounds of -1.3 and +3: this is the term that was most wrong on the costly side, +4.6, outside its bounds, and the loss is 10 to 14 in four profiles of the new head with one or two pieces moved. By the prediction's own sign, waits on `cH`, `cV` or `cEe` over 3 us, the step on SP is at its edge in the first profile (1.7 and 1.2) and wrong in the second, whose waits have these rows:

```profile
PE pe L1110 <- DMA cEe<-rEe: 2.4, 1, 2.4
PE p L320 <- DMA cH<-rH: 2.2, 2, 1.6
```

The bound was made from the two DMA waits of before and one late row group on SP. The new order also puts the first extra product four blocks earlier, and DVE is late for an accumulator: neither was looked at, since the step reasoned about the count of issues and not about when each consumer comes.

*The rivals.* The slower one, `cZ` late in every window, did not happen: the distances of after are 53.74 in all windows. The clock rival did not come at the dense start: the first two X blocks, at 59.02, take 7.13 us, the full pace (two V blocks at 78.22 take 7.03). So the dense part did not begin cold, though transposes were brought forward. The low clock, 0.61 at 48 to 54 us, lies among the small products ahead of it, where before had 1.00.

So, by the two profiles, the forecast ratio was met because a loss of 4.6 us in the head, and a gain of 4.4 in the windows, both unseen, cancel. The kernel after with the old ORDER is 0.9895 and 0.9898 of before: it beats both kernels. The new WINDOW and the serpentine each gain alone; the new head gives some 6 us back, and which of its pieces does so is not shown.

What stays open: why the gains don't add. The new list is worth 8.1 us alone, and 0.9 (974.95 to 974.08, intervals overlapping) where the row products and the serpentine are in. Delays that any of them lets PE catch up would explain it. The distances behind the first one point that way. Under the old list they exceed 53.74 us by 3.2 and 9.9 us in all with eight extra tiles (before, and before with the row products in one), and by 0.0, 0.4 and 0.0 with seven (serpentine, both old lists, old WINDOW). So the serpentine seems to remove the same delay as the new list; this is one profile of each, and no run separates it. New WINDOW and serpentine with the row products of before were not tried together.
